# The fourth channel block's 3x3 convolution on TensorE: nine full-width composed products replaced by a strip projection and sixteen 32x32 products at a time

## The chip, the core and the metric

The kernel runs on one core of one Trainium2 chip. Its engines are TensorE (PE, with its weight loads listed as PEld), VectorE (DVE), ScalarE (ACT), GpSimd (POOL) and SyncE (SP); POOL and SP here mostly issue DMAs, and 16 DMA engines carry them out. The metric is the device time of one execution in microseconds (us); smaller is better. Before the change the median of three runs is 4027.83 us (4027.82 to 4035.51).

## The reference

All data are fp32; x is (16, 128, 96, 96): 16 images, 128 channels, 96 rows of 96 pixels. The block is channel attention and then a convolutional feed-forward part, each with a residual:

```python
xn1 = layernorm_over_channels(x)
q, k, v = xn1 @ wq.T, xn1 @ wk.T, xn1 @ wv.T     # 8 heads of 16 channels
attn = softmax(l2norm(q) . l2norm(k) * 16 ** -0.5)  # 16x16 a head, summed over all pixels
x = x + (attn . v) @ wp.T
xn2 = layernorm_over_channels(x)
h1 = w_in @ xn2                   # 1x1: 128 -> 512 channels
h2 = depthwise_3x3(h1, w_dw)      # each of the 512 channels with its own nine taps, zero padding
x = x + w_out @ gelu(h2)          # 1x1: 512 -> 128 channels
```

## The kernel before

**Units.** An image is cut into 6 bands of 16 rows (`BR`), so there are 96 bands `g`; a band has four units of 4 rows, 384 pixels (`UT`). The 512 hidden channels are four blocks `n` of 128; the fourth is `PE_CHUNK` = 3. The normalised pixels lie channels-first in a ring of rows, `xn`.

**A block of a band through VectorE** (`conv_job`). TensorE makes the hidden channels of up to 18 rows in chunks of 4 or 5 rows (`hidden`, L953), ScalarE copies each chunk with its bias into the padded buffer `h1_n` (`kept`, L956), VectorE applies six taps one after the other, each over the whole band (`tap`, L983), and ScalarE makes the other two taps as scaled copies (`product`, L976), which POOL has the DMA engines add (`add_products`, L990: one DMA adds tap to tap, one adds the sum to VectorE's result). ScalarE then applies the gelu (L994) and hands two rows on to the next band (`halo`, L948).

**The fourth block through TensorE** (`by_matmuls`). In 42 of the 96 bands (`by_pe`, from `PE_SHARE`, `PE_FIRST`, `PE_LAST`) the fourth block is made without `h1`: projection and tap are one 128x128 matrix, `comp[:, t, :]`, and each unit is nine products with shifted windows of `xn` (L1048), accumulated in one PSUM bank. ScalarE applies the gelu with a bias that differs at the left, right, upper and lower edge, so a unit takes three instructions (L1063).

**The last projection** (`ffn_out`, L1083) takes the four blocks of a unit in four accumulating products; ScalarE copies the sum out (L1093) and POOL issues a DMA that adds it to the output. Beside all this run the norms of the next images (transposes L695 and L781, statistics L702 on VectorE, scaling L738 on ScalarE, the gram product L747) and the attention.

**PSUM.** Four banks `h_76` to `h_79` (pool `h`) serve the hidden chunks, the convolution's sums, the projections and the mixes (L644); the transposes have banks of their own (`tr`, `bk`).

**Order.** Nothing is issued in the order of the code. Every step is booked with `op(engine, ns, place, ...)`; `Plan.order` then plays the engines through with the booked lengths and the places (a job number plus an offset from `AT`), and the instructions are written out in the order of their planned starts. Each engine runs its own list strictly in that order.

Of the kernel before, what the change touches and what calls it, by code (L numbers as in the profile page):

```python
# [9 lines left out]
F32 = mybir.dt.float32  # L10
# [12 lines left out]
PE_SHARE = [3, 7]  # L23
PE_LAST = [0, 1, 3]
PE_FIRST = [1, 3, 5]
# [14 lines left out]
    load_1=-26.6, load_2=-35.1, tables=-1.15, weights=-57.1, zeros=54.55, load_a=-138.4, forth_a=-4.3,  # L40
    stats_a=-108.2, variance_a=-56.0, power_a=121.85, scaled_a=-147.25, gram=7.75, back_a=-49.05,
    place_a=-101.15, attention=-134.05, mix=-2.85, residual=-1.05, mixed=-8.2, add_x=322.4, forth_b=-9.4,
    stats_b=-392.95, variance_b=125.25, power_b=7.8, shift_b=-65.25, scaled_b=-188.15, back_b=-7.95,
    place_b=432.7, evicted=147.15, add_out=101.65, halo=222.2, hidden=4.7, kept=-523.7, products=787.25,
    add_last=1.45, tap=114.35, add_first=129.85, gelu=260.5, conv=3.75, conv_gelu=-586.1, out=8.15, add=-76.1,
    store=18.5, mix_0=-315.4, residual_0=432.85, mixed_0=-63.05, add_x_0=4.55, gram_0=-5.3, forth_a_0=-41.9,
    forth_b_0=-8.55, stats_a_0=-27.0, stats_b_0=8.5, scaled_a_0=-384.85, scaled_b_0=188.3, back_a_0=-5.0,
    back_b_0=-35.3, place_a_0=127.65, place_b_0=-16.0, shift_b_0=-104.65, late=322.55, store_x2=-133.3,
    store_x2_0=134.5, variance_a_0=-34.45, variance_b_0=-95.6, power_a_0=-49.25, power_b_0=12.65,
    attention_0=-318.85, load_a_0=-402.4, hidden_0=3.1, kept_0=-35.65, products_0=322.35, tap_0=11.0,  # L50
    add_last_0=26.85, add_first_0=101.1, gelu_0=-0.75, conv_0=2.6, conv_gelu_0=85.7, out_0=6.45,
    evicted_0=-0.95,
)
STEP = dict(scaled=0.3, hidden=0.1, products=0.5, tap=0.166, conv=1.6, conv_tap=0.03, out=0.8, out_part=0.05)
# [11 lines left out]
class Plan:  # L66
# [45 lines left out]
    def order(self):  # L112
# [21 lines left out]
        due, backlog = {}, []  # L134
# [17 lines left out]
        def dispatch(engine, time):  # L152
            queue = queues[engine]
            while queue:
                item = heapq.heappop(queue)
                k = item[1]
                lacks = room(k)
                if lacks is None:
                    break
                waiting.setdefault(lacks, []).append(k)  # L160
            else:
                return
# [36 lines left out]
        def wake(pool, time):  # L199
            for k in waiting.pop(pool, ()):  # L200
                heapq.heappush(queues[ops[k][0]], (ops[k][2], k))
                push(time, "look", ops[k][0])
# [37 lines left out]
def tile_restormer_block(  # L240
# [71 lines left out]
    dw = const.tile([P, NCH, 9], F32, name="dw")  # L312
    ratio = const.tile([P, NCH, 9], F32, name="ratio")
    unit = const.tile([P, NCH], F32, name="unit")
    per_unit = const.tile([P, NCH], F32, name="per_unit")
    beta = const.tile([P, NCH], F32, name="beta")
    edge = const.tile([P, 3, 3], F32, name="edge")
    wvb = const.tile([P, 1], F32, name="wvb")
    ccol = const.tile([P, 2, 2], F32, name="ccol")
    ncq = const.tile([1, P], F32, name="ncq")  # L320
# [6 lines left out]
    comp = const.tile([P, 9, P], F32, name="comp")  # L327
# [11 lines left out]
    h1s = [h1p.tile([P, (BR + 2) * WP + 2], F32, name=f"h1_{n}") for n in range(NCH)]  # L339
# [85 lines left out]

    def zeros(p):

        def around(t):
            r = BR + 2
            nc.gpsimd.memset(t[:, : r * WP].rearrange("p (r w) -> p r w", w=WP)[:, :, :1], 0.0)  # L430
            nc.gpsimd.memset(t[:, r * WP :], 0.0)
# [6 lines left out]
    def weights(p):  # L438
# [8 lines left out]
        def loads_1():  # L447
# [6 lines left out]
            v["w2centre"], v["win_c"] = t[:, 9 * P : 10 * P], t[:, 10 * P : 11 * P]  # L454
            v["sides"] = t[:, 11 * P : 11 * P + 9].rearrange("p (y x) -> p y x", x=3)
# [7 lines left out]
        def loads_2():  # L463
            t = h3_buf(("weights", 0))
            v["win"] = t[:, :HID].rearrange("p (n c) -> p n c", c=P)
            v["wout"] = t[:, HID : 2 * HID]
            nc.sync.dma_start(out=dw, in_=w_dw.rearrange("(n p) o kh kw -> p n (o kh kw)", p=P))
# [42 lines left out]
        def keep_columns():  # L510
# [3 lines left out]
            nc.vector.tensor_scalar(ncq, cqk[:, :P], float(NTOK), None, ALU.mult)  # L514
# [4 lines left out]

        def comp_parts(ts):  # L520
            for t in ts:
                nc.scalar.activation(v["wt"][:, t % 4, :], ident, AF.Copy, scale=ratio[:, PE_CHUNK, t : t + 1])

        def comp_products(ts):
            pt = v["comp"] = bank(("weights", ts))
            for t in ts:
                k = t - ts[0]
                nc.tensor.matmul(
                    pt[:, k * P : (k + 1) * P], lhsT=v["win_c"], rhs=v["wt"][:, t % 4, :], start=True, stop=True
                )  # L530

        def keep_comp(ts):
            nc.scalar.copy(comp[:, ts[0] : ts[-1] + 1, :].rearrange("p t c -> p (t c)"), v["comp"][:, : len(ts) * P])

        def in_centred():
# [4 lines left out]
            nc.tensor.matmul(pb[:, :P], lhsT=winT[:, PE_CHUNK, :], rhs=v["w2centre"], start=True, stop=True)  # L540
# [3 lines left out]
        def keep_in_centred():  # L544
            nc.scalar.copy(winT.rearrange("p n c -> p (n c)"), v["in_a"])
            nc.scalar.copy(v["win_c"], v["in_b"][:, :P])
            nc.scalar.copy(beta, v["in_b"][:, P : P + NCH])

        def edges_of():
# [478 lines left out]
    def by_matmuls(p, g, s):  # L1028
# [7 lines left out]
        def reach(t):  # L1036
            dy = t // 3 - 1
            return max(0, -dy - r0), min(UR, H - r0 - dy)
# [149 lines left out]
```

## Time and profile before

| | |
|---|---|
| runs | 4035.51, 4027.82, 4027.83 us |
| profiled execution | span 4032.2 us, 51195 instructions; the page lists no other time for it |
| PE, DVE, ACT, POOL busy | 3973.7, 3964.5, 3704.6, 1939.2 us |
| DMA | 834.19 MB, mean 207 GB/s |
| granted TensorE clock | 0.997 of full speed |

Busy time of an engine counts overlapping instructions once; the group's mean is that of one instruction from its start to its end, and instructions that follow each other overlap by part of it. So what an instruction takes of its engine is read from the distance of two starts in the timeline. One product of the program on fp32 data stands in the trace as two records (a pass each, with a weight load each: the last projection is 1536 products and 3072 records); a transpose is one. The DMA row is the mean busy share of the 16 DMA engines.

### The profile page before, as it was taken

The page shows a single profiled execution, that of the slowest core. Times are in us where ns is not written, and L with a number is a line of the kernel's source. Part 1 is how long each engine was busy: PE and PEld are TensorE (multiplying, and loading weights), DVE is VectorE, ACT ScalarE, POOL GpSimd, SP SyncE. Part 2 cuts the span into 40 slices and gives each one's busy share as a digit, 9 for nine tenths or more (in the row PEclk, how much of TensorE's full clock was granted, in tenths as well). Part 3 has the DMA queues.
Part 4 walks back from the last instruction along what each step waited for, and adds up shares of the span by engine and source line. Part 5 has one row for each costly group of instructions (what it writes and reads, how often), then busy time and mean ns, then how long its engine had stood idle before and what let it go on. Part 6 is the DMA issues. An engine that isn't in the chain of part 4 may idle for free.

```text
span 4032.2 us, 51195 instructions
## 1 busy us (share of the span) xinstructions
PE 3973.7 (99%) x17048; PEld 2593.8 (64%) x17048; DVE 3964.5 (98%) x3478; ACT 3704.6 (92%) x7676; POOL 1939.2 (48%) x1596
## 2 busy tenths in 40 slices
PE   9999999999999999999999999999999999999989
PEld 7666666666666666666666666666666666666555
DVE  6999999999999999999999999999999999999999
ACT  7999999899999999999999999999999999999985
POOL 4545445454554544545455454544545455454431
PEclk9999999999999999999999999999999999999999
DMA  5999999999999999999999999999999999999997
GB/s 143 211 202 208 195 218 217 193 230 197 216 220 208 216 203 223 213 209 215 203 215 213 202 216 195 233 206 209 227 196 215 214 219 219 205 214 187 202 192 156
DMA packets 197159, 834.19 MB, mean 207 GB/s; under 512 B 22816, under 2 KB 24352, under 8 KB 196896
## 3 DMA queue, kind: packets, MB, share of 16 engines
q0 software_dynamic: 138960, 679.10, 85.9%
q1 hardware_dynamic: 57936, 151.83, 10.4%
q8 instruction: 136, 2.23, 0.2%
q14 instruction: 127, 1.04, 0.1%
HBM read 150.62 MB, written 149.42 MB: 74 GB/s over the span
## 4 chain that ended last, share of the span: by engine, by line
PE 75%; DVE 11%; ACT 8%; DMA 2%; issue 2%; POOL 2%; POOLq 0%; DVEq 0%; ACTq 0%; SPq 0%
PE h L1083 19%; PE h L1048 19%; PE h L953 16%; DVE h L983 10%; PE g L747 6%; PE h L644 4%; PE pB_a L781 3%; PE pT_a L695 3%; PE pB_b L781 2%; PE pT_b L695 2%; ACT h L976 2%; ACT h L956 1%; POOL rstd_b L713 1%; ACT zT L738 1%; DMA x<-in_x_dram 1%
## 5 line engine op out<-in xcount | busy, mean ns | idle before, releaser
L983 DVE SCALAR_TENSOR_TENSOR h<-h,ratio,h 128x1520 f32<-128x1520 f32 (+1 forms) x1712 | 2983.7, 1778 | 6.5
L1083 PE MATMUL h<-h,woutT 128*128 128x384 f32 x3072 | 1131.9, 488 | 4.1 <-ACT h L956 3.6
L976 ACT ACTIVATE h<-h,ratio 128x1536 f32<-128x1536 f32 (+1 forms) x682 | 1090.3, 1610 | 5.6 <-PE h L1083 3.8
L1048 PE MATMUL h<-xn,comp 128*128 128x380 f32 (+5 forms) x3090 | 1074.7, 478 | 4.4 <-ACT h L956 3.7
L953 PE MATMUL h<-xn,winT 128*128 128x384 f32 (+3 forms) x2720 | 1065.5, 494 | 8.6 <-ACT h L956 4.7
L990 POOL DMA_DIRECT2D h<-h x682 | 628.7, 957 | 885.2 <-ACT h L976 399.5
L956 ACT ACTIVATE h<-h,beta 128x384 f32<-128x384 f32 (+1 forms) x1318 | 791.2, 632 | 76.9 <-PE h L953 54.8
L1083 PEld LDWEIGHTS h<-h,woutT 128*128 128x128 f32 x3072 | 554.2, 190 | 335.0 <-issue 36.7
L1048 PEld LDWEIGHTS h<-xn,comp 128*128 128x128 f32 x3090 | 557.2, 191 | 312.5 <-issue 22.2
L713 POOL TENSOR_TENSOR rstd_a<-ve_a,mhalf 128x4 f32<-128x4 f32 x288 | 527.5, 1844 | 447.1 <-ACT ve_a L709 428.0
L713 POOL TENSOR_TENSOR rstd_b<-ve_b,mhalf 128x4 f32<-128x4 f32 x288 | 564.6, 1986 | 351.4 <-ACT ve_b L709 346.2
L953 PEld LDWEIGHTS h<-xn,winT 128*128 128x128 f32 x2720 | 486.1, 190 | 279.8 <-issue 19.8
L983 DVE SCALAR_TENSOR_TENSOR h<-h,ratio 128x1536 f32<-128x1536 f32 x342 | 618.4, 1810 | 5.9 <-ACT h L956 3.2
L994 ACT ACTIVATE h<-h 128x1536 f32<-128x1536 f32 (+1 forms) x345 | 520.7, 1510 | 23.9 <-DMA h<-h 21.4
L738 ACT ACTIVATE zT<-pT_b,rstd_b 128x128 f32<-128x128 f32 x1132 | 329.6, 403 | 35.4 <-POOL rstd_b L713 33.4
L738 ACT ACTIVATE zT<-pT_a,rstd_a 128x128 f32<-128x128 f32 x1080 | 316.5, 411 | 4.8 <-POOL rstd_a L713 3.7
L747 PEld LDWEIGHTS g<-zT 128*128 128x128 f32 x2160 | 275.0, 191 | 42.8 <-ACT zT L738 0.9
L644 PE MATMUL h<-xn,mwT 128*128 128x384 f32 x768 | 296.2, 490 | 5.5 <-ACT h L1063 2.1
L656 POOL DMA_DIRECT2D x<-in_x_dram x189 | 182.1, 967 | 237.4 <-ACT x L653 166.6
L747 PE MATMUL g<-zT 128*128 128x129 f32 x2160 | 285.5, 274 | 0.3 <-ACT zT L738 0.3
L653 ACT ACTIVATE x<-h,d 128x384 f32<-128x384 f32 x378 | 227.1, 637 | 11.2 <-PE h L644 4.3
L781 PEld LDWEIGHTS pB_b<-ident,zT 128*128 128x128 f32 x1152 | 147.0, 142 | 111.0 <-issue 52.2
(185 smaller groups left out, 3226.3 us busy)
## 6 DMA issues: line engine op xcount, KB each, us to landing
h<-h POOLq DMA_DIRECT2D x569, 768.0 KB, 10.0
h<-h POOLq DMA_DIRECT2D x113, 720.0 KB, 13.2
x<-in_x_dram SPq DMA_DIRECT2D x192, 384.0 KB, 8.2
out_dram<-x SPq DMA_DIRECT2D x190, 384.0 KB, 9.9
x<-in_x_dram POOLq DMA_DIRECT2D x189, 384.0 KB, 10.7
out_dram<-h POOLq DMA_DIRECT2D x94, 768.0 KB, 10.3
out_dram<-x SPq DMA_DIRECT2D x4, 192.0 KB, 1.9
h<-in_L_conv_w_in_dram SPq DMA_DIRECT2D x1, 256.0 KB, 6.3
```

The costliest lines, as they stand in the source:

```text
L644: nc.tensor.matmul(rows(pm), lhsT=mats[i][0], rhs=interior(i, u), start=True, stop=True)
L713: nc.gpsimd.tensor_tensor(rstd, d["ve"], mhalf, ALU.pow)
L738: nc.scalar.activation(zT(q)[:, k, :P], d["pT", q][:, k, :], AF.Copy, scale=d["rstd"][:, t : t + 1])
L747: nc.tensor.matmul(grams[i][:, : P + 1], lhsT=zt[:, :P], rhs=zt, start=(q == 0 and k == 0), stop=(q == NU * TPU // QT - 1 and k == QT - 1),)
L953: nc.tensor.matmul(rows(ph)[:, k : k + m, :], lhsT=winT[:, n, :], rhs=z, start=True, stop=True)
L956: nc.scalar.activation(window(h1_, r, e - r, 1), rows(d.pop(("ph", r))), AF.Identity, bias=beta[:, n : n + 1])
L976: nc.scalar.activation(d["pr", t][:, o0:o1, :], shifted(t, o0, o1), AF.Copy, scale=ratio[:, n, t : t + 1])
L983: nc.vector.scalar_tensor_tensor(h3[:, o0:o1, w0:w1], shifted(t, o0, o1, w0, w1), ratio[:, n, t : t + 1], onto, ALU.mult, ALU.add)
L990: nc.gpsimd.dma_start(out=to[:, o0:o1, :], in_=d["pr", t][:, o0:o1, :], accum_op=ALU.add)
L994: nc.scalar.activation(h3, h3, AF.Gelu)
L1048: nc.tensor.matmul(d["pc"][:, o0 + k : o0 + k + m, w0:w1], lhsT=comp[:, t, :], rhs=z[:, :, w0 + dx : w1 + dx], start=(t == order[0]), stop ...
L1083: nc.tensor.matmul(rows(d["po"]), lhsT=woutT[:, n, :], rhs=h3s[g, n][:, s * UR : (s + 1) * UR, :], start=(k == 0), stop=(k == NCH - 1),)
```

## The change

71 of the 96 bands have their fourth block made on TensorE, and they do it in another way. The changed `by_matmuls` works on a whole band at a time, in three stages.

- **split.** For each group k of 32 hidden channels, the projection is made of four column strips of the image (24 columns and one more on each side, 26 x 18 = 468 places), each a product with 128 rows and 32 columns of weights that writes the partitions 32q to 32q+31 of one bank. Places outside the image get minus the bias from a small product of `nbeta` with a row of ones (L1074). Two banks are filled in one step; there are two such steps a band.
- **packed.** ScalarE copies each bank into the buffer of the fourth block, which now has the shape of four such packs (L1081).
- **conv.** For each tap, sixteen products with 32x32 diagonal weights (`taps`): strip q lies on partitions 32q, channel group k goes to partitions 32k of bank q. All four banks of pool `h` are held from the first tap to the last. ScalarE then makes one gelu a bank (L1099) with one bias, `whole`.

`taps`, `whole` and `nbeta` are made once at the start (they replace `comp` and `edge`). The four products of `ffn_out` become one step, so nothing is put between them. The pads of the fourth block's buffer are set again when the bands change from TensorE to VectorE (`around`, 24 more pairs of small POOL memsets). `Plan.order` keeps a step that waits for banks from being overtaken by later ones of its engine that want the same pool. All places in `AT` are new.

```diff
-PE_SHARE = [3, 7]
-PE_LAST = [0, 1, 3]
-PE_FIRST = [1, 3, 5]
+PE_SHARE = [3, 4]
+PE_LAST = [0, 1, 3, 4]
+PE_FIRST = [1, 2, 4, 5]
...
                 lacks = room(k)
                 if lacks is None:
+                    lacks = next((t[0] for t in ops[k][5] if item > ahead.get((t[0], engine), item)), None)
+                if lacks is None:
                     break
...
+        def diagonals():
+            nc.vector.tensor_copy(v["by_part"], v["spread"].rearrange("p (g t) -> p g t", t=10))
+            for t in range(9):
+                for g in range(4):
+                    nc.vector.tensor_scalar(taps[:, t, g, :], v["eye"], v["by_part"][:, g, t : t + 1], None, ALU.mult)
...
-    def by_matmuls(p, g, s):
+    def by_matmuls(p, g):
...
-                nc.tensor.matmul(
-                    d["pc"][:, o0 + k : o0 + k + m, w0:w1], lhsT=comp[:, t, :], rhs=z[:, :, w0 + dx : w1 + dx],
-                    start=(t == order[0]), stop=(t == order[-1] and k == got[-1][0]),
-                )
...
+            for e, m, z in pieces(i, r0 - 1 + k0, k1 - k0):
+                for q in range(4):
+                    c0 = q * (W // 4) - 1
+                    lo, hi = max(c0, 0), min(c0 + SW, W)
+                    to = strips(ph[q * Q : (q + 1) * Q, :])[:, k0 + e : k0 + e + m, lo - c0 : hi - c0]
+                    nc.tensor.matmul(to, lhsT=winT[:, PE_CHUNK, w], rhs=z[:, :, lo:hi], start=True, stop=True)
+            for to in sides:
+                nc.tensor.matmul(to, lhsT=nbeta[:, w], rhs=ones_row[:, : to.shape[1]], start=True, stop=True)
...
+        def kept(k):
+            nc.scalar.copy(packed(k), strips(d.pop(("ph", k))))
+
+        def conv():
+            for q in range(4):
+                d["pc", q] = bank((g, "conv", q), BR * W // 4)
+            for t in range(9):
+                dy, dx = divmod(t, 3)
+                for q in range(4):
+                    qs = slice(q * Q, (q + 1) * Q)
+                    for k in range(4):
+                        nc.tensor.matmul(
+                            d["pc", q][k * Q : (k + 1) * Q, :].rearrange("p (r w) -> p r w", w=W // 4),
+                            lhsT=taps[qs, t, k, :], rhs=packed(k)[qs, dy : dy + BR, dx : dx + W // 4],
+                            start=(t == 0), stop=(t == 8),
+                        )
+
+        def gelu(q):
+            to = h3_of(g, PE_CHUNK)[:, :, q * (W // 4) : (q + 1) * (W // 4)]
+            nc.scalar.activation(to, d["pc", q].rearrange("p (r w) -> p r w", w=W // 4), AF.Gelu, bias=whole)
```

What this does to the order on **PE** is seen in a band of the tenth image before (`comp`: the fourth block's products; `pB`, `pT`, `g`: transposes and gram of the norms):

```order
L1048 MATMUL h_78<-xn,comp 128x384
L781 MATMUL pB_b_8_16478<-ident,zT_152 128x128 x3
L695 MATMUL pT_a_0_16482<-ident,x_0_15680 128x128 x4
L1048 MATMUL h_78<-xn,comp 128x4x95 x4
L1048 MATMUL h_78<-xn,comp 128x384
L1048 MATMUL h_78<-xn,comp 128x4x95
L1083 MATMUL h_79<-h_3_139,woutT 128x384
```

The nine products of a unit use one bank, and other work stands between them. After the change, PE just ahead of a convolution of the twelfth image and at its head (the first four of its 36 rows):

```order
L970 MATMUL h_79<-xn,winT 128x288
L970 MATMUL h_79<-xn,winT 128x96
L710 MATMUL pT_b_13_28066<-ident,x_11_8_27224 128x128 x2
L710 MATMUL pT_b_13_28066<-ident,x_11_9_27508 128x128 x2
L762 MATMUL g_27209<-zT_150 128x129 x4
L796 MATMUL pB_a_14_28082<-ident,zT_149 128x128 x2
L796 MATMUL pB_a_14_28082<-ident,zT_150 128x128
L1091 MATMUL h_77<-h_3_132,taps 32x384 x4
L1091 MATMUL h_79<-h_3_132,taps 32x384 x4
L1091 MATMUL h_78<-h_3_132,taps 32x384 x4
L1091 MATMUL h_76<-h_3_132,taps 32x384 x4
```

Transposes and the gram product now stand between the last use of a bank and the convolution, which then runs as one block of 144 products over all four banks. Behind its last row:

```order
L1091 MATMUL h_79<-h_3_132,taps 32x384 x4
L796 MATMUL pB_a_15_28253<-ident,zT_150 128x128 x3
L710 MATMUL pT_a_13_28257<-ident,x_8_27799 128x128 x2
L710 MATMUL pT_a_13_28257<-ident,x_9_27924 128x128 x2
L762 MATMUL g_27209<-zT_149 128x129 x4
L970 MATMUL h_77<-xn,winT 128x384
```

Again transposes and gram stand where no bank is free yet; the next hidden chunk takes the bank whose gelu comes first. On **ACT**, around a convolution of the same image (L993: products of another block, L1011: its gelu, L753: scaling of the norm, L668 and L799: other copies):

```order
L799 COPY xn<-pB_b_1_26806 128x384
L753 ACTIVATE zT_148<-pT_b_2_26755,rstd_b_2_26802 128x128 x4
L724 ACTIVATE ve_b_3_26976<-st_b_3_26971 128x4
L993 ACTIVATE h_0_133<-h_2_131,ratio 128x1536
L1011 ACTIVATE h_6_139<-h_6_139 128x1536
L753 ACTIVATE zT_149<-pT_b_3_26813,rstd_b_3_26979 128x128 x4
L993 ACTIVATE h_10_143<-h_2_131,ratio 128x1440
L1099 ACTIVATE h_2_135<-h_77,whole 128x16x24
L799 COPY xn<-pB_b_2_26991 128x384
L1099 ACTIVATE h_2_135<-h_76,whole 128x16x24
```

Work that needs no bank of pool `h` is put beside the convolution; the first gelu is the row at which ScalarE waits for it.

More of the change, by code (lines that the diff above doesn't have):

```diff
@@ L45 @@
[L45 to L49, printed above, removed]
@@ new lines @@
+    gram=-98.35, back_a=-1104.8, place_a=-162.8, attention=-147.0, mix=-235.0, residual=-1.05, mixed=-1161.85,
+    add_x=-251.1, forth_b=-185.9, stats_b=321.8, variance_b=542.1, power_b=-166.2, shift_b=-65.25,
+    scaled_b=1255.35, back_b=-1583.4, place_b=243.75, evicted=-1337.25, add_out=196.2, halo=6.6, hidden=202.7,
+    kept=-141.7, products=3263.6, add_last=118.65, tap=748.85, add_first=1317.75, gelu=3239.45, split=205.1,
+    packed=1185.5, conv=-517.6, conv_gelu=-941.25, out=208.8, add=1006.25, store=278.9, mix_0=-343.8,
@@ L55 @@
+    add_last_0=-24.6, add_first_0=-3.4, gelu_0=692.1, split_0=-9.0, packed_0=303.35, conv_0=195.15,
+    conv_gelu_0=-258.8, out_0=116.4, evicted_0=-422.5,
+)
+RESERVE = True
+Q = 32
+STEP = dict(scaled=0.657, hidden=0.086, products=0.594, tap=0.259, split=0.046, out=-0.806)
 SLACK = dict(PE=450, DVE=120, ACT=130, POOL=410, ADD=200, MOVE=360)
@@ L199, in wake @@
         def wake(pool, time):
+            for engine in queues:
+                ahead.pop((pool, engine), None)
             for k in waiting.pop(pool, ()):
@@ new lines, in by_matmuls, with split @@
+        parts = [[("h1", PE_CHUNK, e)] for e in range(4)]
+        parts[0] += [("h1", PE_CHUNK, e) for e in ("first", "last", *range(4, 7))]
+        def split(k):
+            ph = d["ph", k] = bank((g, "split", k), PART)
+            w = slice(k * Q, (k + 1) * Q)
+            k0, k1 = 1 if r0 == 0 else 0, BR + 1 if r0 + BR == H else BR + 2
+            sides = []
+            for q in range(4):
+                to = strips(ph[q * Q : (q + 1) * Q, :])
+                if k0:
+                    sides.append(to[:, 0, :])
+                if k1 < BR + 2:
+                    sides.append(to[:, k1, :])
+                if q in (0, 3):
+                    sides.append(to[:, k0:k1, SW - 1 if q else 0])
+            for e, m, z in pieces(i, r0 - 1 + k0, k1 - k0):
[6 more added lines that the diff above has]
+                nc.tensor.matmul(to, lhsT=nbeta[:, w], rhs=ones_row[:, : to.shape[1]], start=True, stop=True)
@@ L1074, in ffn_out @@
+        pcs = [("h", (g, "conv", c)) for c in range(4)]
+        h3 = [("h3", (g, PE_CHUNK), s) for s in range(UPB)]
+        pe(9 * t_mm(BR * W // 4) + 480, at("conv", p, g >= HEAD), conv, [*sum(parts, []), ("w", "conv")], [*pcs, ("pk",), *h3])
+        for c in range(4):
+            act(t_act(UT, 1) - 43, at("conv_gelu", p, g >= HEAD), lambda c=c: gelu(c), [pcs[c]], h3)
     def ffn_out(p, g, s):
@@ L1078, in ffn_out, with products @@
         order = sorted(range(NCH), key=lambda n: (n != PE_CHUNK, n))
-        def product(k, n):
-            if k == 0:
-                d["po"] = bank(("out", g, s), UT)
-            nc.tensor.matmul(
-                rows(d["po"]), lhsT=woutT[:, n, :], rhs=h3s[g, n][:, s * UR : (s + 1) * UR, :],
-                start=(k == 0), stop=(k == NCH - 1),
-            )
+        def products():
+            d["po"] = bank(("out", g, s), UT)
+            for k, n in enumerate(order):
+                nc.tensor.matmul(
+                    rows(d["po"]), lhsT=woutT[:, n, :], rhs=h3s[g, n][:, s * UR : (s + 1) * UR, :],
+                    start=(k == 0), stop=(k == NCH - 1),
+                )
         def add_here():
```

189 lines of the change are left out of this document (88 added, 101 removed).

## The prediction

> **What bounds the kernel now.** I read the busy shares first, then the chain of work that ended last, then the busy time by stretches, and last the DMA queues.
>
> ```profile
> PE 3973.7 (99%) x17048; PEld 2593.8 (64%) x17048; DVE 3964.5 (98%) x3478; ACT 3704.6 (92%) x7676; POOL 1939.2 (48%) x1596
> PE 75%; DVE 11%; ACT 8%; DMA 2%; issue 2%; POOL 2%; POOLq 0%; DVEq 0%; ACTq 0%; SPq 0%
> 0.00:100.00 100.00, 91.06 (x543) 71.21 (x544) 64.51 (x154) 71.50 (x203) 41.89 (x76) 0.98 0.54 143
> 100.00:2000.00 1900.00, 1883.91 (x8173) 1234.68 (x8172) 1889.03 (x1635) 1783.10 (x3712) 934.54 (x751) 1.00 0.98 210
> 2000.00:3900.00 1900.00, 1870.88 (x7940) 1213.85 (x7939) 1885.49 (x1612) 1768.80 (x3644) 942.91 (x747) 0.99 0.99 210
> 3900.00:4032.00 132.00, 127.83 (x396) 74.10 (x394) 125.46 (x80) 81.16 (x122) 19.86 (x23) 0.99 0.76 158
> q0 software_dynamic: 138960, 679.10, 85.9%
> q1 hardware_dynamic: 57936, 151.83, 10.4%
> q8 instruction: 136, 2.23, 0.2%
> q14 instruction: 127, 1.04, 0.1%
> ```
>
> In the four stretches the columns after the colon are length, PE, PEld, DVE, ACT and POOL busy, granted clock, DMA share, GB/s. The chain runs mostly over PE, but three resources are full at once: from 100 to 3900 us DVE is busy 3774.5 of 3800 us, PE 3754.8, and the DMA engines 98 to 99%. ACT has some 7% left. So the time falls only as far as the **fullest of DVE, PE and DMA** falls, and I make one sum for each. DVE leaves 68 us of the span idle (4032.2 - 3964.5), PE 58. The four DMA queues sum to 96.6% of the span, 3895 us, which leaves 137: some 46 in the first 100 us, 32 in the last 132, the rest spread.
>
> **DVE.** Its work is taps:
>
> ```profile
> L983 DVE SCALAR_TENSOR_TENSOR h<-h,ratio,h 128x1520 f32<-128x1520 f32 (+1 forms) x1712 | 2983.7, 1778 | 6.5
> L983 DVE SCALAR_TENSOR_TENSOR h<-h,ratio 128x1536 f32<-128x1536 f32 x342 | 618.4, 1810 | 5.9 <-ACT h L956 3.2
> ```
>
> 3602 us for 2054 taps is 1.754 us each. 71 bands for 42 take 29 blocks from DVE, six taps each: 174 x 1.754 = 305 us. The some 40 small operations that build the diagonals fall into the first 100 us, where DVE is busy 64.5; I cost them at nothing. With the same idle time DVE would end at 4032 - 305 = **3727**.
>
> **DMA.** The same 29 blocks take 58 adds with them, and the order has them as 49 whole ones and 9 of an image's top or bottom band (569 to 520, 113 to 104):
>
> ```profile
> h<-h POOLq DMA_DIRECT2D x569, 768.0 KB, 10.0
> h<-h POOLq DMA_DIRECT2D x113, 720.0 KB, 13.2
> ```
>
> Queue q0 takes 0.859 x 4032 = 3464 us for 679.1 MB, 5.10 us a MB. A whole add is 0.786 MB, 4.01 us, the other 0.737 MB, 3.76 us: 49 x 4.01 + 9 x 3.76 = 230 us. Against that, PE's program grows: q8 brings 2.23 MB in 0.2% of the span, 8 us, for 17048 pairs of records; 21644 products, all but 4608 transposes in two passes, are 38680 pairs, 2.27 times as many: 10 us more. With the same idle time DMA would end at 4032 - 230 + 10 = **3812**; with the 59 us of spread idle gone, at 3753. This is the largest of the three sums, and the change does less for it than for the others.
>
> **PE.** The pitch of a pass is the distance of two starts:
>
> ```profile
> 2012.12 1.45 PE L1048 MATMUL h<-xn,comp 128*128 128x384 f32 x4
> 2013.41 0.97 PE L953 MATMUL h<-xn,winT 128*128 128x480 f32 x2
> 2014.22 0.81 PE L1083 MATMUL h<-h,woutT 128*128 128x384 f32 x2
> 2014.86 0.97 PE L953 MATMUL h<-xn,winT 128*128 128x480 f32 x2
> ...
> 45.24 0.36 PE L865 MATMUL h<-ones,wide 128*128 128x1 f32 x2
> 45.46 0.36 PE L864 MATMUL h<-gs,wqkT 128*128 128x1 f32 x2
> ...
> L1048 PE MATMUL h<-xn,comp 128*128 128x380 f32 (+5 forms) x3090 | 1074.7, 478 | 4.4 <-ACT h L956 3.7
> L953 PE MATMUL h<-xn,winT 128*128 128x384 f32 (+3 forms) x2720 | 1065.5, 494 | 8.6 <-ACT h L956 4.7
> ```
>
> Four passes of 384 columns take 1.29 us (2012.12 to 2013.41), 0.3225 each; one of 480 takes 0.405; so 0.84 ns a column. Two passes of a single column still take 0.22 us: there the weight load of 128 columns is what is left, 0.11.
>
> Removed: 42 bands x 36 products x 2 passes x 0.32 = 968 us, and 29 hidden blocks, by the order 48,300 columns less, twice 0.84 ns: 81 us. PE without the fourth block on TensorE is 3974 - 968 - 81 = 2925.
>
> Added: no row shows products in parts of the array, so the conv has bounds. If sixteen stream together, a band is 9 taps x 2 x 0.3225 = 5.8 us. If its 288 weight loads come one after another and a load of 32 columns takes a quarter of 0.11 us, they need 7.9 us. If a load costs 0.11 however narrow it is, 31.7. If nothing overlaps, 288 x 0.3225 = 92.9. Today weight loads hide behind products (PEld is busy 64% and PE does not wait for it), so I stay at the lower end and take the middle of 5.8 and 7.9: 6.9 us, 71 x 6.9 = 490. The split, with four strips streaming together, is 4 x 2 x 0.395 (468 of 480 columns) = 3.2 us a band, 224. The 936 side products have few columns; two loads of a quarter of 0.11 each make 51 us (206 at the full 0.11). PE: 2925 + 490 + 224 + 51 = 3690; with its 58 idle it would end at **3748** (3619 with a conv of 5.8 and sides that cost nothing).
>
> [...]
>
> **ACT** gains little:
>
> ```profile
> 2013.61 0.89 ACT L1063 ACTIVATE h<-h,edge 128x376 f32<-128x376 f32 x3 [0.49 <-PE h L1048]
> 2014.42 0.66 ACT L956 ACTIVATE h<-h,beta 128x480 f32<-128x480 f32 x1
> ...
> 2018.87 0.60 ACT L653 ACTIVATE x<-h,d 128x384 f32<-128x384 f32 x1
> 2019.33 0.50 ACT L784 COPY xn<-pB_b 128x384 f32<-128x384 f32 x1
> ...
> 2021.45 0.46 ACT L1093 COPY h<-h 128x384 f32<-128x384 f32 x1
> 2021.81 0.48 ACT L784 COPY xn<-pB_b 128x384 f32<-128x384 f32 x1
> ...
> 2022.29 1.57 ACT L976 ACTIVATE h<-h,ratio 128x1536 f32<-128x1536 f32 x1
> 2023.75 1.05 ACT L653 ACTIVATE x<-h,d 128x384 f32<-128x384 f32 x2
> ...
> 2028.12 1.60 ACT L994 ACTIVATE h<-h 128x1536 f32<-128x1536 f32 x1
> 2029.51 0.76 ACT L956 ACTIVATE h<-h,beta 128x480 f32<-128x480 f32 x1
> ```
>
> A band on PE took 4 x 0.81 = 3.2 us; now four copies of 468 (0.36 us for 384, so 0.44) and four gelus at the 0.46 of an activation of 384 from PSUM make 3.6. A block on DVE took two products at 1.46, a gelu at 1.39 and some 1.8 of copies: 6.1. 71 x 3.6 - 42 x 3.2 - 29 x 6.1 = -56: ACT needs 3649 and would be 96% busy at 3800, for 92 now. It is not the bound, but it has little left to catch up with.
>
> **New waits.** The conv needs all four banks. Ahead of it stand transposes and gram in the order, some 1.65 us (4 x 0.11 + 4 x 2 x 0.11 + 3 x 0.11), against 0.8 for the last bank's copy (the 0.16 by which a product outlasts its pitch, and 0.60); behind it the same kinds cover the first gelu. I cost these at nothing while ACT is on time. Without the cover it would be 0.8 and 0.8 a band, and the wait for an instruction that ACT has in front, up to 1.46: 2.9 us, 71 x 2.9 = 206. At ACT the first gelu waits for the conv, and copies of the norms queue behind it; they feed PE and the ring. The 24 pairs of pad memsets go to POOL, which is busy 48%.
>
> **The sum.** DVE 3727, PE 3748, DMA 3812. Since DVE and PE have more room than now, adds are issued a little earlier, and some of the spread DMA idle should close: I take 10 of the 59 us. 3802 on the profiled execution's clock; its span lies 4.4 us over the median of the runs, so **3798 us**, 5.7% faster. Its own range is 3740 (DMA idle closed) to 3850 (PE some 100 us over its sum).
>
> **Rivals.**
> - *The sixteen do not fully overlap.* With a conv over 7.7 us PE passes DMA's sum; at 10.9 it uses up the whole gain ((3974 - 2925 - 224 - 51) / 71). In the middle, 9.3 us: 2925 + 660 + 275 + 58 = 3918. For it: the one-column rows show that a load is not free. Against: loads of different parts may go side by side.
> - *Banks.* The covers fail because ACT, at 96%, is late: 3748 + 206 = 3954. For it: four banks are all there are, and one conv takes them 71 times. Against: PE's idle before L953 and L1083 today is 8.6 and 4.1 us in all.
> - *It does not do what it says: the passes of a tile run in order, and the next tile queues behind them.* Each product is two passes on one tile. If the second starts only when the first has streamed, and the following tile's first must start after it, at most two tiles run at once: 144 x 0.3225 = 46.4 us a conv, 16 x 0.395 = 6.3 a split. PE: 2925 + 71 x 52.7 + 51 + 58 = 6776, **slower**. It decides from 10.9 us a conv, that is from fewer than some nine tiles at once. For it: in every row of the trace a pass starts when the one before has streamed. Against: all of those use the whole array and could not do otherwise. A load that costs 0.11 at any width belongs here too: 2925 + 2251 + 275 + 58 = 5509.
>
> [...]
>
> **Chances.** The forecast 0.62; overlap short of sixteen 0.10; banks 0.08; slower 0.18 (third rival, nearly all of it far above 5000); no change 0.02. A measurement of this kernel can tell about 0.2% from no change; so faster 0.80, same 0.02, slower 0.18. The range 3735 to 4000 takes in the forecast's own range and the first two rivals; the slow case stays out.
>
> **What would show it.** Right: a conv whose 288 passes start within 6 to 8 us; 1880 taps, some 3300 us on DVE; 58 adds fewer and a DMA share of 98 to 99% between the ends; idle before the first L1091 product near nothing. Wrong: passes of a conv 0.16 or 0.32 us apart; ACT waiting at L1099; DMA below 95% in the middle, since then something else holds the end.

## The result and the profile after

The changed kernel takes **4252.73 us** (median of 4 runs, 4248.14 to 4267.31) against 4027.82 of the kernel before: 1.0561 times as long, 95% interval 1.0537 to 1.0584. The forecast was 3798. The profiled execution spans 4246.4 us, with a mean granted clock of 0.960 (0.997 before).

From the page of the changed kernel: the busy times, three DMA queues and the chain by engine.

```profile
PE 3945.6 (93%) x38648; PEld 2537.3 (60%) x38648; DVE 3693.3 (87%) x3339; ACT 3630.5 (85%) x7473; POOL 1836.1 (43%) x1586
...
q0 software_dynamic: 130608, 633.92, 77.9%
q1 hardware_dynamic: 57936, 151.83, 10.0%
q8 instruction: 304, 4.98, 0.4%
...
PE 75%; ACT 14%; issue 6%; DVE 4%; POOL 1%; DMA 1%; DVEq 0%; POOLq 0%; ACTq 0%
```

Its busy time in the two long stretches (columns as in the prediction: length, PE, PEld, DVE, ACT, POOL, granted clock, DMA share, GB/s):

```profile
100.00:2000.00 1900.00, 1768.53 (x17347) 1135.57 (x17348) 1659.49 (x1463) 1648.31 (x3403) 847.60 (x705) 0.96 0.89 189
2000.00:3900.00 1900.00, 1779.07 (x17821) 1149.60 (x17820) 1651.50 (x1455) 1646.53 (x3404) 840.51 (x704) 0.96 0.90 189
```

In the middle no resource is full: DVE was busy 3774.5 of 3800 us and is now busy 3311, the DMA engines fell from 98 to 99% to 89 to 90%. PE is the fullest with 3547.6, and it too has 252 us of gaps. "issue" in the chain has grown from 2 to 6% of the span: time in which PE waited for nothing that the profile shows. Three of the page's groups say where:

```profile
L1000 DVE SCALAR_TENSOR_TENSOR h<-h,ratio,h 128x1520 f32<-128x1520 f32 (+1 forms) x1567 | 2736.0, 1781 | 8.7
...
L1091 PE MATMUL h<-h,taps 32*32 32x384 f32 x20448 | 663.1, 533 | 200.1 <-issue 193.5
...
L1000 DVE SCALAR_TENSOR_TENSOR h<-h,ratio 128x1536 f32<-128x1536 f32 x313 | 566.0, 1812 | 119.4 <-ACT h L973 118.9
```

So do the longest waits of PE and of those that wait for it (us in total, times, longest):

```profile
PEld h L1091 <- issue: 299.0, 260, 5.0
ACT h L1099 <- PE h L1091: 295.2, 72, 10.8
...
PE h L1091 <- issue: 193.5, 77, 4.3
DVE st_a L717 <- PE pT_a L710: 192.5, 53, 8.2
```

PE stops at L1091 for 200 us, nearly all of it "issue". ACT's 295 us at L1099 and DVE's waits for PE are what that does to the others. One conv in the timeline of PE (start, length, and the idle time before in brackets):

```profile
1939.05 6.17 PE L1091 MATMUL h<-h,taps 32*32 32x384 f32 x224
1947.35 2.65 PE L1091 MATMUL h<-h,taps 32*32 32x384 f32 x64 [2.13 <-issue]
1949.93 0.90 PE L796 MATMUL pB_a<-ident,zT 128*128 128x128 f32 x3
```

The DMA queues from 1944.9 to 1946.0, around the start of its pause (packets, MB, share of the engines' time):

```profile
q0 software_dynamic: 51, 0.22, 100.6%
q8 instruction: 1, 0.02, 5.5%
```

And the busy time before, in and behind the pause:

```profile
1936.00:1945.20 9.20, 9.20 (x239) 6.02 (x237) 9.09 (x8) 9.20 (x18) 5.77 (x5) 1.00 0.75 169
1945.30:1947.30 2.00, 0.00 (x0) 0.00 (x0) 0.22 (x1) 0.35 (x1) 1.01 (x2) 1.00 1.03 209
1947.98:1951.38 3.40, 3.40 (x55) 2.04 (x39) 0.00 (x0) 1.10 (x3) 0.14 (x2) 0.50 1.01 206
```

224 of the conv's 288 passes start, then PE stands still for 2.1 us, loads no weights either, and goes on with the other 64. From 1944.9 to 1946.0 one packet of queue q8, that of PE's instructions, is in the DMA engines, which are full of data (q0 at 100%). By the trace's records the packet starts at 1944.95 and has landed at 1945.92; PE goes on 1.43 us later. And from 1947.98 on, for 3.4 us, the granted clock is 0.50: **this pause of 2.1 us is followed by 3.4 us at half the clock**.

This is the pattern of 66 of the 71 convs. Worked out from the records (a pause is a gap of over 0.1 us between one product's end and the next one's start):

| conv in the changed kernel | |
|---|---|
| 71 convs, from first to last record | 863.2 us, 12.16 each |
| convs with no pause at the full clock | 5, of 7.85 to 8.16 us, mean 7.96 |
| pauses | 86, 200.1 us; in 48 convs one, in 16 two, in 2 three |
| where the pauses stand | counting loads, products and semaphore events along PE's list: 78 of the 86, 193.6 us, at the same place in 256 instructions, within one; the other eight, 6.5 us, behind the first 16 products of a conv |
| two pauses of one conv at that place | 128 products lie between them, in all 13 cases |
| an instruction packet | 4.98 MB / 304 = 16.4 KB; 4.98 MB by the 2 x 38648 products and loads is 64 bytes each: 256 instructions, 128 products with their loads |
| from a landing to the end of such a pause | 1.42 us (median; 1.23 to 1.56 for nine in ten) |
| half clock | 59 stretches of 3.4 to 13.7 us, 338 us (before: 7, 27 us); 58 begin in a PE gap or within 4 us of its end; 163.5 us lie within convs, 138 of them over running products |

The row on the place is the strongest: if the products themselves paused, there would be no reason for one place in 256 of the whole list. The 193.6 us are also, almost to the digit, the 193.5 us that the profile calls "issue". Of the 71 convs, which all pass two or three such places, 65 pause at one.

So theory **F**: a conv is 576 instructions, 2.25 packets, and uses up a packet in 3.3 us. The packets arrive later than that, in part since they wait behind data in the DMA engines (tested in e2); PE stands still, and around a pause the clock is halved. The rivals were that the sixteen products have a slow pace of their own, and **O**, that the new order, made for a conv booked at 6.28 us, is to blame.

### The profile page after: what moved, and what is told of

It reads as the page before. It is cut to its first block, busy times and chain, and to the rows that moved or that the text cites. A ratio compares the mean times of both kernels' runs of the same rounds, so it can differ in the third digit from the quotient of the medians.

```text
span 4246.4 us, 93678 instructions
## 1 busy us (share of the span) xinstructions
PE 3945.6 (93%) x38648; PEld 2537.3 (60%) x38648; DVE 3693.3 (87%) x3339; ACT 3630.5 (85%) x7473; POOL 1836.1 (43%) x1586
## 3 DMA queue, kind: packets, MB, share of 16 engines
q8 instruction: 304, 4.98, 0.4%
## 4 chain that ended last, share of the span: by engine, by line
PE 75%; ACT 14%; issue 6%; DVE 4%; POOL 1%; DMA 1%; DVEq 0%; POOLq 0%; ACTq 0%
PE h L1123 19%; PE h L1091 15%; PE h L970 14%; PE g L762 5%; PE h L659 4%; PE h L1072 4%; DVE h L1000 3%; ACT h L993 3%; PE pB_a L796 3%; ACT h L973 2%; PE pB_b L796 2%; PE pT_a L710 2%; PE pT_b L710 2%; ACT zT L753 2%; ACT h L1011 2%
## 5 line engine op out<-in xcount | busy, mean ns | idle before, releaser
L1000 DVE SCALAR_TENSOR_TENSOR h<-h,ratio,h 128x1520 f32<-128x1520 f32 (+1 forms) x1567 | 2736.0, 1781 | 8.7
L993 ACT ACTIVATE h<-h,ratio 128x1536 f32<-128x1536 f32 x624 | 1012.0, 1643 | 0.1
L970 PE MATMUL h<-xn,winT 128*128 128x384 f32 (+3 forms) x2486 | 936.1, 501 | 7.8 <-ACT h L1081 7.0
L1091 PE MATMUL h<-h,taps 32*32 32x384 f32 x20448 | 663.1, 533 | 200.1 <-issue 193.5
L973 ACT ACTIVATE h<-h,beta 128x384 f32<-128x384 f32 (+1 forms) x1204 | 700.1, 656 | 25.7 <-PE h L970 16.7
L1091 PEld LDWEIGHTS h<-h,taps 32*32 32x32 f32 x20448 | 384.5, 107 | 424.2 <-issue 299.0
L1011 ACT ACTIVATE h<-h 128x1536 f32<-128x1536 f32 (+1 forms) x316 | 487.3, 1543 | 14.8 <-DVE h L1000 8.7
L717 DVE BATCH_NORM_STATS2 st_a<-pT_a 128x6 f32<-128x256 f32 x540 | 204.3, 421 | 259.8 <-PE pT_a L710 192.5
L1099 ACT ACTIVATE h<-h,whole 128x384 f32<-128x384 f32 x284 | 164.9, 590 | 295.4 <-PE h L1091 295.2
L753 ACT ACTIVATE zT<-pT_b,rstd_b 128x128 f32<-128x128 f32 x1132 | 337.2, 428 | 6.1 <-POOL rstd_b L728 6.1
L753 ACT ACTIVATE zT<-pT_a,rstd_a 128x128 f32<-128x128 f32 x1080 | 328.3, 451 | 12.7 <-POOL rstd_a L728 12.4
L799 ACT COPY xn<-pB_a 128x384 f32<-128x384 f32 x384 | 208.9, 544 | 102.9 <-PE pB_a L796 98.0
L717 DVE BATCH_NORM_STATS2 st_b<-pT_b 128x6 f32<-128x256 f32 x566 | 213.0, 420 | 86.8 <-PE pT_b L710 53.1
```

The source lines that it names most:

```text
L753: nc.scalar.activation(zT(q)[:, k, :P], d["pT", q][:, k, :], AF.Copy, scale=d["rstd"][:, t : t + 1])
L970: nc.tensor.matmul(rows(ph)[:, k : k + m, :], lhsT=winT[:, n, :], rhs=z, start=True, stop=True)
L973: nc.scalar.activation(window(h1_, r, e - r, 1), rows(d.pop(("ph", r))), AF.Identity, bias=beta[:, n : n + 1])
L993: nc.scalar.activation(d["pr", t][:, o0:o1, :], shifted(t, o0, o1), AF.Copy, scale=ratio[:, n, t : t + 1])
L1000: nc.vector.scalar_tensor_tensor(h3[:, o0:o1, w0:w1], shifted(t, o0, o1, w0, w1), ratio[:, n, t : t + 1], onto, ALU.mult, ALU.add)
L1011: nc.scalar.activation(h3, h3, AF.Gelu)
```

## The experiments

All are the changed kernel with one edit; e7 and e8 have all places anew as well. e1, e2 and e5 leave out part of what the block computes and ran once. In the table, conv and pauses are worked out as above, the conv's mean over its bands (in e6 and e8 its busy time and pauses, without the rows put between); "at packet ends" are the pauses at the one place in 256; "half clock" is the sum of the stretches at 0.5.

| | time, us | to before | conv, us | pauses, us | at packet ends, us | half clock, us |
|---|---|---|---|---|---|---|
| the change | 4252.73 | 1.0561 | 12.16 x 71 | 200 | 194 | 338 |
| e1, four taps | 3883.5 (one run) | | 4.07 x 71 | 8 | 0 | 172 |
| e2, no adds | 4030.9 (one run) | | 9.63 x 71 | 73 | 67 | 140 |
| e3, longer booking | 4296.57 | 1.0675 | 11.26 x 71 | 147 | 133 | 325 |
| e4, 42 bands | 4372.49 | 1.0869 | 13.97 x 42 | 158 | 94 | 615 |
| e5, half the products | 3904.1 (one run) | | 6.86 x 71 | 15 | 8 | 107 |
| e6, in parts | 4208.12 | 1.0374 | 11.19 x 71 | 106 | 98 | 198 |
| e7, 49 bands, new places | 4085.69 | 1.0139 | 12.66 x 49 | 132 | 121 | 329 |
| e8, e7 in parts | 4089.09 | 1.0149 | 12.33 x 49 | 85 | 49 | 281 |
| e9, one pass a product | 3924.31 | 0.9750 | 2.90 x 71 | 49 | 34 | 411 |

The kernel before took 4024 to 4028 us on the chips of these runs, and 4051 on that of e5 and e6; ratios are to it.

**e1: four taps of nine.**

```diff
-            for t in range(9):
+            for t in range(4):
-                            start=(t == 0), stop=(t == 8),
+                            start=(t == 0), stop=(t == 3),
```

> The conv makes only four of its nine taps (64 products, 128 passes with 128 weight loads, 256 instructions, for 576); the order and all else stay, so the fourth block's result lacks five taps in 71 bands. Theory F (PE runs out of instructions: its program comes in packets of 16 KB, 256 instructions, one packet ahead, and a conv uses a packet up in about 3.3 us, sooner than the next one arrives): a conv of 256 instructions crosses at most about one packet, which was asked for long before, so the waits of L1091 for issue fall from 193 us to under 20, the half-clock time from 338 us to under 70, and a conv takes 3.8 to 4.0 us, without outliers. Theory P (the pauses come from the 32x32 products themselves, their tiles or weight loads): pauses per product stay, so some 86 us of waits for issue, and a conv of some 5.4 us. The span ends on DVE or DMA in both, 3750 to 3850.

From e1's page, the busy times and the conv's group:

```profile
PE 3592.2 (93%) x27288; PEld 2282.6 (59%) x27288; DVE 3684.3 (95%) x3339; ACT 3618.6 (93%) x7473; POOL 1868.3 (48%) x1586
...
L1091 PE MATMUL h<-h,taps 32*32 32x384 f32 x9088 | 281.3, 500 | 7.5 <-ACT h L973 3.9
```

And its first long stretch:

```profile
100.00:2000.00 1900.00, 1766.33 (x13444) 1120.12 (x13443) 1815.55 (x1602) 1800.73 (x3720) 936.50 (x772) 0.98 0.97 206
```

At four taps a conv is 256 instructions, one packet, and passes one packet's end: none of the 71 pauses there. The idle time of L1091 falls from 200.1 to 7.5 us (waits for ACT and others), and 59 of 71 convs run clean, in some 3.64 us. Pauses do not fall with the number of taps (200 x 4/9 would be 89), they vanish, as F says. The half clock (172 us) and the span (3882, above 3850) were expected lower. With the conv nearly gone as a cost, the time still does not reach the forecast; the DMA engines are back at 97%.

**e2: the adds are planned but not issued**, so the DMA engines carry 306 MB for 792.

```diff
-            nc.gpsimd.dma_start(out=to[:, o0:o1, :], in_=d["pr", t][:, o0:o1, :], accum_op=ALU.add)
+            _ = to
```

> The 624 DMAs that add the two ScalarE taps are not issued, so these taps are missing in the result of 313 blocks; PE's list and program are the same. The DMA engines' share falls from 88% to some 35%. Theory F, with the instruction packets waiting behind data in the DMA engines: the waits of L1091 for issue fall from 193 us to under 80, conv without pauses become the rule (5 of 71 now), the half-clock time halves at least, and the span falls to 3850 to 4050, PE's own need. Theory F with a fixed latency of a packet: 193 us stay within 30, span 4150 to 4250. Theory P: the same as the fixed latency.

From e2's page and list of groups, the busy times, the conv's group and the queue that carried the adds:

```profile
PE 3854.9 (96%) x38648; PEld 2500.5 (62%) x38648; DVE 3689.7 (92%) x3339; ACT 3622.1 (90%) x7473; POOL 1255.0 (31%) x962
...
L1091 PE MATMUL h<-h,taps 32*32 32x384 f32 x20448 | 610.6, 505 | 73.1 <-issue 67.0 <-ACT h L973 4.0 <-ACT x L668 1.9
...
q0 software_dynamic: 40752, 148.26, 22.3%
```

PE executes the same 38648 passes. With queue q0 at 22% for 78 the pauses fall to 73 us, and 25 convs run clean at full clock where 5 did (not yet the rule, as F expected). So the pauses depend on the data in the DMA engines: with less of it a packet starts sooner, as the next numbers show. They do not vanish. From the point 256 instructions ahead of a pause at a packet's end, the packet starts 4.1 us later in the changed kernel and 3.1 us later here (medians), and PE goes on 6.5 and 5.4 us after that point. Even with the engines two thirds empty (DMA share 0.35 in the middle) a packet comes slower, 5.4 us, than the 3.3 us in which a conv uses one up. The span is what PE's shorter time makes of it: 4246 - (863 - 684) for the convs - (174 - 89) / 2 for the half clock outside them = 4024, measured 4029. **PE is the bound of the changed kernel**, and the conv is why.

**e3: the conv booked at 11.0 us instead of 6.28**, so that the order is planned with about the time it takes.

```diff
-        pe(9 * t_mm(BR * W // 4) + 480, at("conv", p, g >= HEAD), conv, [*sum(parts, []), ("w", "conv")], [*pcs, ("pk",), *h3])
+        pe(11000, at("conv", p, g >= HEAD), conv, [*sum(parts, []), ("w", "conv")], [*pcs, ("pk",), *h3])
```

> The plan books 11.0 us for a conv, near its measured mean of 12, in place of 6.3; everything that is computed stays, only the order is laid out anew. Theory O (the loss is an order laid out for too short a conv, so ACT waits 295 us at the first gelu and POOL and DVE behind it): with a fitting order at least half of the excess goes, below 4100 us. Theory F (PE has no more than 100 us of idle time beside the instruction waits, so its own list is the bound): 4180 to 4280, with the waits at L1099 mostly gone and the waits for issue still near 193.

Slower still: 1.0675 (1.0657 to 1.0693), though the convs themselves take 63 us less. A booking nearer to the truth does not help, so O in the form "the order is planned for too short a conv" falls. F's own range for this run (up to 4280) was missed too, by 17 us, and ACT still waits 228 us at L1099, where F had that wait mostly gone.

**e4: the 42 bands of before (`PE_SHARE = [3, 7]`, `PE_LAST = [0, 1, 3]`, `PE_FIRST = [1, 3, 5]`) with the new conv.**

> The new conv in 42 of the 96 bands, as many as before the change, in the new order. Theory F: PE loses 29 bands at some 14 us (12.2 conv, 3.9 split, 1.2 half clock outside, less 2.8 for the hidden chunks), 4246 - 400 = 3840, so DVE and DMA are the bound again as before the change: 4025 to 4070, the same as before within 1%. Theory O, or a new order that is worse by itself: 4100 or more.

A miss: 4372, slower than with 71 bands, and all engines have gaps (PE 87% busy, DVE 91%, ACT 85%). The places were found for 71 bands; with another share the same places leave idle time everywhere. It says that the order decides much when the share changes. By its own terms it falls on the side of "a new order that is worse by itself"; on the pauses it cannot decide, though 94 of its 158 us still stand at packets' ends. e7 repeats the question with places of its own.

**e5: half the products.** Of the four channel groups, two get all nine taps and two the centre tap alone, so 80 products for 144 and eight at a time.

```diff
-                    for k in range(4):
+                    for k in range(4 if t == 4 else 2):
-                            start=(t == 0), stop=(t == 8),
+                            start=(t == (0 if k < 2 else 4)), stop=(t == (8 if k < 2 else 4)),
```

> The conv makes two of its four channel groups in all taps and the other two in the centre tap alone: 80 products of 144, 160 passes, 320 instructions; half of the fourth block's channels lack eight taps. The same 18 rounds stream one after another, eight tiles in a round for sixteen. A conv without pauses takes 7.95 us now, 0.42 us a round where 384 columns need 0.3225. If the round is bound by its sixteen weight loads one after another (0.026 us each), eight loads hide behind the streaming and a clean conv takes 18 x 0.32 + 0.2 + 0.48 = 6.3 to 6.7 us; if a round of parts of the array costs 0.42 us however many tiles it has, 7.9 to 8.0 us. Theory F (instructions come late): 256 instructions last 4.7 us for 3.3 us, so the waits for issue at L1091 fall from 193 us to 20 to 80; theory P (pauses by product): 107 us.

From e5's page, the busy times and the conv's group:

```profile
PE 3740.8 (96%) x29560; PEld 2379.7 (61%) x29560; DVE 3688.1 (95%) x3339; ACT 3614.9 (93%) x7473; POOL 1875.4 (48%) x1586
...
L1091 PE MATMUL h<-h,taps 32*32 32x384 f32 x11360 | 472.6, 488 | 14.6 <-issue 8.1
```

A clean conv takes 6.36 us here, with 320 instructions: a packet lasts 5.1 us, where the change uses one up in 3.3. Of the 71 convs 47 pass a single packet's end, and none of them pauses there; of the 24 that pass two, 10 do. The waits for issue, 8.1 us, are below even F's range of 20 to 80. The clean conv also gives the pace of the products: a tap of eight products takes (6.36 - 0.48 - 0.83) / 8 = 0.63 us, two streams of 0.32; a tap of sixteen 7.5 / 9 = 0.83 in a clean conv of the change (the last product of a conv outlasts its pitch by some 0.48). So sixteen overlap well, though not fully.

**e6: the conv in parts** of three, two, two and two taps; after each, PE's next transposes or gram that need no bank of pool `h` may go ahead.

```diff
-        def conv():
-            for q in range(4):
-                d["pc", q] = bank((g, "conv", q), BR * W // 4)
-            for t in range(9):
+        def conv(ts=range(3)):
+            if not ts[0]:
...
+                parted[:] = [lambda: conv(range(3, 5)), lambda: conv(range(5, 7)), lambda: conv(range(7, 9))]
+            for t in ts:
...
         for work in plan.order():
             work()
+            if parted and work in free_of_banks:
+                parted.pop(0)()
```

> Everything is computed as in the changed kernel; only PE's list differs: the conv is issued in four parts of three, two, two and two taps, and the next bank-free rows of PE's list (transposes and gram, mostly 0.33, 0.43 and 0.88 us) stand between the parts instead of behind them. Theory F: these rows need few instructions and give the next packet up to 1.6 us more time, so the waits for issue at L1091 fall from 193 us to 60 to 140, half-clock time from 338 us to 180 to 290, and the span to 4080 to 4200 us. If the pauses come from the products themselves, or the order decides: no change, 4225 to 4275.

The conv's group on e6's page (its line is L1101 there):

```profile
L1101 PE MATMUL h<-h,taps 32*32 32x384 f32 x20448 | 688.4, 514 | 106.1 <-issue 98.2
```

And the wait of its gelus, from the list of waits:

```profile
ACT h L1111 <- PE h L1101: 343.6, 77, 9.8
```

The same products and the same instructions, spread over more time: idle time at the conv halves (200.1 to 106.1), the half clock falls from 338 to 198 us, and the ratio from 1.0561 to 1.0374 (1.0341 to 1.0407). The intervals do not touch. The direction is F's, though the span is 8 us above F's range. The gain is small: the conv still needs its 2.25 packets, and ACT waits longer for a conv that ends later (343.6 us for 295.2); how much each of these costs was not taken apart.

**e7: 49 bands, with all places searched anew for them**, the conv booked at 11.3 us.

```diff
-PE_SHARE = [3, 4]
+PE_SHARE = [1, 2]
-PE_FIRST = [1, 2, 4, 5]
+PE_FIRST = [1, 3, 5]
...
-        pe(9 * t_mm(BR * W // 4) + 480, at("conv", p, g >= HEAD), conv, [*sum(parts, []), ("w", "conv")], [*pcs, ("pk",), *h3])
+        pe(11300, at("conv", p, g >= HEAD), conv, [*sum(parts, []), ("w", "conv")], [*pcs, ("pk",), *h3])
```

> The new conv (all 144 products) for 49 or 50 bands instead of 71, and every place in the order found anew for that number, with a conv booked at 11300 ns. This asks what e4 could not, since e4 kept places made for 71 bands. F (instruction packets late, clock lowered behind the pauses): each band that leaves PE frees 12.16 us of conv, 3.9 us of split and sides and some 2.4 us of half clock, so PE falls from after's 4246 to about 4246 - 21 x 18.4 = 3860, VectorE rises by 21 x 6 taps x 1.754 = 221 to about 3950, and the end is set by the order: 4010 to 4080 us, with 50 x 2.8 = 140 us of pauses inside the convs and under 300 us at half clock. If instead the new conv costs too much wherever it stands (only undoing it helps), PE stays the bound, over 95% of the span, and the time is over 4150.

**e8: e7 with the parts of e6.**

> e7 with the conv issued in parts of 3, 2, 2 and 2 taps with PE's next bank-free rows between them, as in e6. F: as e6 against after (4208 against 4253, half clock 198 against 338 us), less by the share of the convs: 20 to 40 us under e7, 3980 to 4050, with half clock under 200 us. If e6's gain came only from PE being the bound there, e8 equals e7 within 10 us, since in e7 the order sets the end.

From e7's page, the busy times and the conv's group (L1161 there), and e8's conv from its list of groups:

```profile
PE 3772.4 (92%) x31084; PEld 2417.8 (59%) x31084; DVE 3910.9 (96%) x3471; ACT 3680.9 (90%) x7451; POOL 1851.6 (45%) x1672
...
L1161 PE MATMUL h<-h,taps 32*32 32x384 f32 x14112 | 488.4, 555 | 131.9 <-issue 120.6
...
L1171 PE MATMUL h<-h,taps 32*32 32x384 f32 x14112 | 519.2, 547 | 85.2 <-issue 49.4 <-POOL h L513 22.6 <-ACT h L1051 13.2
```

e7 ends at 4085.69, 6 us above its range and far from the 4150 of the other theory: with fewer bands PE is no longer the bound, DVE is (96%). Per conv nothing has changed (12.66 us, 2.7 us of pauses each), and no conv runs clean. e8 more than halves the waits for issue (120.6 to 49.4 us) and ends where e7 does, 4089.09: F's range for it, 20 to 40 us less, was missed, and the other branch came out, that e6's gain came from PE being the bound. Idle time of PE costs little once DVE is the fullest. The half clock, expected under 300 and 200, was 329 and 281. Neither comes down to the kernel before. Before, 42 bands cost PE 968 us in products; these 49 cost 620 in convs and some 185 in the split, by the distances of starts. So PE has some room here, but DVE's taps stay: six for each of 335 blocks, where there were 342.

**e9: one pass a product.** The packed strips and the diagonals are kept as float16. That rounds the conv's two inputs to 11 bits; the sums stay float32.

```diff
+F16 = mybir.dt.float16
-    taps = const.tile([P, 9, NCH, Q], F32, name="taps")
+    taps = const.tile([P, 9, NCH, Q], F16, name="taps")
-        return strips(h1s[PE_CHUNK][:, k * PART : (k + 1) * PART])
+        return strips(h1s[PE_CHUNK].bitcast(F16)[:, k * PART : (k + 1) * PART])
```

> after with the conv's operands (the packed strips and the diagonals of taps) kept as float16, so the conv's inputs are rounded to 11 bits; its sums stay float32 and nothing else changes. All 144 products of a conv stay, but each is one load and one product in place of two: 288 PE instructions a conv instead of 576, 1.1 packets of 256 instead of 2.25. F (instruction packets late): conv at 144 pairs x 26 ns = 3.7 us plus 0.5, some 4 to 5.5 us with pauses, pauses in all under 40 us (after: 200), half clock under 200 us, and the time as with four taps of nine (e1: 3883): 3860 to 3930 us. A theory in which sixteen products at a time are slow by themselves (start one after another, or collide in their banks) leaves the number of products as it was and so at least half of the conv's excess: convs of 7 us or more, over 4000 us.

From e9's page, the busy times and the queue of PE's instructions:

```profile
PE 3549.0 (90%) x28424; PEld 2301.1 (59%) x28424; DVE 3687.5 (94%) x3339; ACT 3630.6 (92%) x7473; POOL 1835.0 (47%) x1586
...
q8 instruction: 224, 3.67, 0.4%
```

The conv's group in e9's list of groups (L1092 there):

```profile
L1092 PE MATMUL h<-h,taps 32*32 32x384 f16 x10224 | 156.8, 337 | 49.1 <-issue 33.9 <-ACT x L669 5.8 <-ACT h L974 5.6
```

And its first long stretch:

```profile
100.00:2000.00 1900.00, 1724.09 (x13851) 1117.15 (x13852) 1794.95 (x1583) 1785.04 (x3675) 911.73 (x763) 0.95 0.96 204
```

DVE and the DMA engines are the fullest again, 94 and 96% in this stretch. All 144 products stay and each is one load and one pass: 288 instructions, 1.1 packets. 40 of 71 convs run clean, in 1.9 to 2.2 us, the mean is 2.90, and the kernel takes **3924.31 us, 0.975 (0.9737 to 0.9764) of the kernel before**: faster than both, by computing one of four channel blocks of 71 bands with inputs of less precision. A conv was expected at 4 to 5.5 us, pauses under 40 (49 measured, 34 of them at packets' ends) and half clock under 200 (411 measured). By itself e9 does not part F from a slow pace, since a pass is shorter too (13 ns from start to start, below, for 26); e2 and e6, with the same passes, do. Its clean 2 us bears on the pace: 144 float16 loads and products start within it, some 13 ns apart, so products can start closer together than the 26 ns of the float32 passes (7.5 us / 288).

## Why the prediction was wrong

**The step that failed is the price of the conv**: "I stay at the lower end and take the middle of 5.8 and 7.9: 6.9 us, 71 x 6.9 = 490". It measured 12.16 us, 863 in all. Of a conv's 12.16 us, 7.96 are its clean pace, which lies at the upper end of that bound, 2.82 are pauses (200.1 / 71) and 0.97 half clock over running products (138 / 2 / 71; in it the conv's products start 46 ns apart on average for 26 at the full clock, the passes of the last projection 0.64 us for 0.32, so the half is an estimate). Some 0.4 is left; that the product before a pause outlasts its pitch, as the last of a conv does by some 0.48, could be this (an estimate). Bounds made of streams and weight loads held; what was left out was whether the instructions are there. The prediction saw the growth of queue q8 and had its size right (2.23 MB x 2.27 = 5.06; 4.98 measured), but entered it as 10 us of load on the DMA engines. Their 4.98 MB take 0.4% of the span; **that they come late costs PE 194 us, and the halved clock around the pauses comes on top**. The division that would have shown it: 2.25 packets a conv of 6.9 us is a packet in 3.1 us, where the kernel before took one in 30 us (4032 / 136). What it needs stood in the prediction's own rows: 2.23 MB in 136 packets is 16.4 KB each, and by 2 x 17048 products and loads 65 bytes each, so some 250 instructions a packet (an estimate from these rows; the pauses show 256).

**With that price, its own sums come out.** PE's sum, 3748, with 863 for 490 is 4121; the half clock outside the convs, (338 - 163.5) / 2 = 87 at most, makes 4208. The span is 4246. The other terms were near: at the full clock, by the distances of starts, the split with its sides cost 260 us (275 taken), and the hidden chunks 75 us less than before (81 taken). The decision point was right: "at 10.9 it uses up the whole gain". At 12.16 PE alone is slower than before.

**A second error was hidden behind it: the sum for the end.** In e5 the conv happens to measure 6.86 us, the very price that was taken, and PE is busy 3741 us (3690 predicted, and half of 107 us of half clock). Yet the span is 3902, not 3802. e1 and e9, with convs of 4.07 and 2.90, end at 3882 and 3930. So below 7 us the conv no longer decides, and in this order, with DVE and DMA 94 to 97% busy in the middle of these runs, the end comes some 80 to 130 us after the forecast's 3802. "With the same idle time" was the assumption: the DMA queues left 137 us idle before and leave 171 in e1 (their four shares sum to 95.6% of 3881.7). Of the 444 us between forecast and span (4246 - 3802), e5 puts 344 on the conv and 100 on this; roughly, since on e5's chip the kernel before took 24 us longer.

**What held.** DVE's taps: 1880 in 2736 + 566 = 3302 us, predicted some 3300. The adds: 520 + 104 = 624, 58 fewer. Two of the three signs that were named for a wrong forecast appear: ACT waiting at L1099 (295 us), and DMA below 95% in the middle (89 to 90%). ACT did not become the bound: its wait is a consequence, and in e1 the idle time at the conv is 7.5 us with ACT at 93%, so the rival of the banks did not occur. (Its price was added up 0.16 us a band too low: 0.8 + 0.8 + 1.46 is 3.06, not 2.9.)

**The rivals.** The case that came out is slower, but by none of the mechanisms that were priced. The third rival, passes in order, is refuted: 288 passes in 7.96 us for 92.9 one after the other is 11.7 at a time, where the lower bound had 16. Here products of different tiles did not wait for each other's stream: 26 ns lie between two starts (7.5 us / 288), and a stream of 384 columns is 0.3225 us in the rows of before. The first rival's conv, 7.7 to 10.9 us, holds for the clean pace, and is not what decided.

**What stays open.** Why e3 and e4 are slower than F alone gives: their idle time is spread over all engines, and no run took it apart. When exactly a packet is requested stands in no row. Over the changed kernel, the packet that PE needs at such a place of its list starts between 4.9 us before and 7.4 us after PE passes the place 256 instructions earlier, and PE never goes on past a place sooner than 1.07 us after the landing. This fits a request of one packet ahead that then waits.

## What to carry to other kernels

Where small products replace large ones, count instructions per microsecond beside streams and loads: divide by the 256 that a packet of 16.4 KB held here, and ask whether the packets, behind the data of a full DMA queue, come that fast; here one needed 5.4 to 6.5 us. Count the packets' ends that a dense stretch passes, too: of the 178 convs of e1, e5 and e9 that passed one, 5 paused at it; of the 71 of the change, which passed two or three, 65 did. Prefer fewer passes (a narrower type, eight tiles instead of sixteen: pauses of 49 us in e9 and 15 in e5, for 200) to a denser packing that starves; other work between the small products helped less (e6, 106 us). And where three resources are equally full, the largest of their sums is only a lower bound for the end: here the runs without the packets' pauses ended 80 to 130 us above it.

## What the hardware showed

- **PE gaps and the clock.** Of 68 PE gaps of over 2 us in the changed kernel 52 have a half clock that begins in them or within 4 us of their end; of 76 between 0.2 and 1 us, 3; between 1 and 2 us, 7 of 37. The half stretches are 3.41 us or multiples of it, but for the last. In e9 it is 60 of 70 gaps over 2 us, and 32 of 65 between 1 and 2 us. Of the 42 gaps of 2 to 3 us in the changed kernel 27 are among the 52.
- **The half clock is not the packets' alone.** e9 has 49 us of pauses in its convs and 411 us of half clock, around PE's other gaps. PE is busy 90% there; what the half clock costs the span was not shown.
- **Sixteen 32x32 tiles.** A tap's two passes take 0.83 us in float32 (0.645 if sixteen streamed together), eight tiles 0.63, and one pass of sixteen in float16 some 0.19 to 0.2 (1.9 / 9 less the last product's tail).
